# Turning the quantized rows of a feed-forward layer by DMA instead of on TensorE

## The chip, the cores and the metric

The kernel runs on one core of a Trainium2 chip. A core has TensorE (PE, matrix products; its weight loads are listed apart as PEld), VectorE (DVE), ScalarE (ACT), GpSimd (POOL), and SyncE (SP), which here only issues DMAs. The metric is the device time of one execution in microseconds, as a median over runs.

## The reference

Two layers act on an array x of 8 x 256 rows of 512 numbers, each as an attention and a feed-forward with a residual:

```
x = x + attention0(layernorm(x), ctx, ctx)
x = x + ffn0(layernorm(x), w1, w2, w3)        # the stage of this change
x = x + attention1(layernorm(x), ctx, ctx)
x = x + experts1(layernorm(x))                # 32 experts, 4 per row, and a shared one
```

ffn0 is a feed-forward whose activations are rounded to 8-bit integers, row by row, and whose weights are rounded to -1, 0 and 1:

```
act_quant(x)    : scale = 127 / max(|x| over the row); round(x * scale), clipped, / scale
weight_quant(w) : scale = 1 / mean(|w|);  round(w * scale) clipped to -1..1, / scale
bitlinear(x, w) = act_quant(x) @ weight_quant(w).T
ffn0(x) = bitlinear(silu(bitlinear(x, w1)) * bitlinear(x, w3), w2)
```

w1 and w3 lead from 512 to 1408 columns, w2 leads back from 1408 to 512.

## The kernel before

The 2048 rows are 16 tiles of 128 rows (`NT` is 16), rows on the partitions. All of x stays in SBUF in 16 tiles `X[i]`. A product on TensorE contracts over the partitions, so the rounded rows of a tile must be turned (their columns put on the partitions, in blocks of 128) before each of the two products of the feed-forward.

`layer0_attention` (lines 196 to 398) first does the attention of layer 0, tile by tile, in the loop at line 377. In its last two rounds it already starts the feed-forward of the first two tiles: `ffn_input` (416) and `ffn_turned` (432), whose results go into `g.begun`. Its PSUM pool `a0ps` fills all eight banks; the tag `t`, one bank, takes the transposes.

`ffn_input(i)` normalizes tile i of x (`xn`, line 424) and rounds it. `quantize` (401) does this in four steps: maximum of each row on DVE (406), its scale and the inverse of it (408, 410), scaling and rounding on ACT by adding a large constant (411), and on DVE the subtraction of that constant with a cast to bf16 (412). The result is `xq`, 128 x 512, with the scales `s13`.

`ffn_turned` turns `xq` in four blocks by `transpose_blocks` (104): one TensorE transpose per block (108) into PSUM, then one ACT copy (436) into `xqT` in SBUF, of which there are three buffers.

`layer0_ffn` (440 to 486) is the loop over tiles. `hidden` makes the 1408 columns in three chunks of 512, 512 and 384: for each chunk four products with w1 into `p1` and four with w3 into `p3` (453), Silu on ACT (457), and the product of the two on DVE (458) into `h`. Then `quantize` rounds `h` to `hq`, 128 x 1408 in bf16. `output` turns `hq` in eleven blocks by TensorE into two PSUM tiles, copies them by ACT (472) to `hqT`, multiplies with w2 in eleven products into `py` (475), and adds the result to x (476).

The PSUM pool `f0ps` has two buffers each of `p1`, `p3`, `py` and `t`, eight banks together.

The loop at line 480 is written in the order hidden(n-2), output(n-4), ffn_turned(n): two tiles lie between a tile's input and its hidden part, and two between that and its output. The order on each engine is not exactly the written one. A planner orders the instructions ahead of time: on each engine, what is ready by its reckoning and stands first in the written order goes next, and buffers that are still in use hold an instruction back. It is free to take instructions of the next stage early: so the norms of layer 1 (`layernorm`, 67, called at 573) and loads for later stages (`load_early`, 1121, on SP's queue) appear within this stage. Once ordered, each engine and each queue works strictly in order.

Of the kernel before, what the change touches and what calls it, by code (L numbers as in the profile page):

```python
# [19 lines left out]
F32 = mybir.dt.float32  # L20
BF16 = mybir.dt.bfloat16
# [9 lines left out]
P = 128  # L31
D = 512
KD = D // P
# [3 lines left out]
NT = T // P  # L37
# [4 lines left out]
FF = 1408  # L42
NF = FF // P
# [60 lines left out]
def transpose_blocks(g, pool, src, n, dtype, ident, tag):  # L104

    pt = pool.tile([P, n, P], dtype, tag=tag, name="pt")
    for k in range(n):
        g.nc.tensor.transpose(pt[:, k, :], src[:, k * P : (k + 1) * P], ident)
    return pt
# [86 lines left out]
def layer0_attention(g, tc, cp, qpool):  # L196


    nc = g.nc
# [4 lines left out]
    with ExitStack() as ctx:  # L204
        wp = ctx.enter_context(tc.tile_pool(name="a0w", bufs=1, reuse_waits="tile"))
        work = ctx.enter_context(tc.tile_pool(name="a0work", bufs=2, reuse_waits="tile"))
        ps = ctx.enter_context(tc.tile_pool(name="a0ps", bufs=1, space=PSUM, reuse_waits="tile"))
# [5 lines left out]
        for c in range(NCH):  # L213
            for i in range(c * CH // P, (c + 1) * CH // P):
                nc.sync.dma_start(out=g.X[i], in_=g.x[i * P : (i + 1) * P, :])
            nc.sync.dma_start(
                out=g.ctxT[c],
                in_=g.ctxT_d[:, c * CH : (c + 1) * CH].rearrange("(k p) t -> p k t", p=P),
# [93 lines left out]
        def gate(i):  # L312
            c, o = divmod(i * P, CH)
            pw = ps.tile([P, D], F32, tag="pq", name="pw", bufs=2)
            for k in range(KD):
                nc.tensor.matmul(  # L316
                    pw, lhsT=xnT[c][:, k, o : o + P], rhs=wg[:, k, :], start=k == 0, stop=k == KD - 1
                )
            return pw
# [7 lines left out]
        def centered(i):  # L327


            raw = work.tile([P, D], F32, tag="raw", name="raw")  # L330
            nc.sync.dma_start(out=raw, in_=g.ctx[i * P : (i + 1) * P, :])
            by_head = raw.rearrange("p (h d) -> p h d", d=HD1)
            mean = g.small.tile([P, H1], F32, tag="mean", name="mean")
            nc.vector.tensor_reduce(mean, by_head, AX.X, ALU.add)
            nc.vector.tensor_scalar(mean, mean, 1.0 / HD1, None, ALU.mult)
            nc.gpsimd.tensor_sub(by_head, by_head, mean.unsqueeze(2).to_broadcast([P, H1, HD1]))
            nc.gpsimd.memset(by_head[:, :, HD1 - 1 :], 1.0)
            nc.gpsimd.dma_start(out=g.vc_d[i * P : (i + 1) * P, :], in_=raw)

        def attended(i):  # L340

            b, j = divmod(i, 2)
            v = V[b]
            po = ps.tile([P, D], F32, tag=f"s{j}", name="po")
            for h in range(H0):
                cols = slice(h * HD0, (h + 1) * HD0)
                late = AT[h][:, S:] if j else g.ones[:, :P]
                nc.tensor.matmul(
                    po[:, cols], lhsT=AT[h][:, j * P : (j + 1) * P], rhs=v[0][:, cols], start=True, stop=False
                )  # L350
                nc.tensor.matmul(po[:, cols], lhsT=late, rhs=v[1][:, cols], start=False, stop=True)
            y = work.tile([P, D], F32, tag="y", name="y")
            layernorm(g, y, po, g.eps["gn"])
            nc.gpsimd.tensor_mul(y, y, gam)
            nc.gpsimd.tensor_add(y, y, bet)
            return y

        def gated(pw, y):
            wy = work.tile([P, D], F32, tag="wy", name="wy")
            nc.vector.scalar_tensor_tensor(wy, pw, 0.0, y, ALU.max, ALU.mult)  # L360
            return wy

        def turned(wy):
            wyT = work.tile([P, KD, P], F32, tag="wyT", name="wyT")
            nc.scalar.copy(wyT, transpose_blocks(g, ps, wy, KD, F32, g.ident, "t"))  # L365
            return wyT
# [10 lines left out]
        for i in range(NT + 1):  # L377
            if i < NT:
                y = attended(i)
                centered(i)  # L380
            if i:
                wyT = turned(wy.pop(i - 1))
            if i == NT - 1:
                g.begun.append(ffn_turned(g, ps, *begun))
            if i < NT:
                wy[i] = gated(pw, y)
            if i + 1 < NT:
                pw = gate(i + 1)
            if i:
                output(i - 1, wyT)  # L390
            if i == NT:
                g.begun.append(ffn_turned(g, ps, *begun))
            if NT - 2 <= i < NT:
                begun = ffn_input(g, work, i - NT + 2)
            if i % 2 and i // 2 + 2 < B:
                for j in range(2):
                    values(i // 2 + 2, j)
            ternary.round()
# [17 lines left out]
def ffn_input(g, work, i):  # L416

    nc = g.nc
    if i % 4 == 0:
        group = g.rs[:, i : i + 4]  # L420
        nc.scalar.activation(group, g.mv[:, i : i + 4, 1], AF.Sqrt, bias=g.eps["ln"])
        nc.vector.reciprocal(group, group)
    xn = work.tile([P, D], F32, tag="y", name="xn")
    nc.vector.tensor_scalar(xn, g.X[i], g.mv[:, i, 0:1], g.rs[:, i : i + 1], ALU.subtract, ALU.mult)
    xq = work.tile([P, D], BF16, tag="xq", name="xq")
    ix = quantize(g, xq, xn, xn)
    s13 = g.fin.tile([P, 2], F32, tag="s13", name="s13", bufs=4)
    nc.vector.tensor_scalar(s13, g.iw[:, :2], ix, None, ALU.mult)
    return xq, s13


def ffn_turned(g, ps, xq, s13):

    pt = transpose_blocks(g, ps, xq, KD, BF16, g.identb, "t")
    xqT = g.fin.tile([P, KD, P], BF16, tag="xqT", name="xqT", bufs=3)
    g.nc.scalar.copy(xqT, pt)  # L436
    return xqT, s13[:, 0:1], s13[:, 1:2]


def layer0_ffn(g, tc):  # L440
    nc = g.nc
    w1, w3, w2 = g.wq
    chunks = [(c, min(c + 512, FF)) for c in range(0, FF, 512)]
    with tc.tile_pool(name="f0work", bufs=2, reuse_waits="tile") as work, tc.tile_pool(name="f0ps", bufs=2, space=PSUM, reuse_waits="tile") as ps:

        def hidden(i, xqT, s1, s3):
            h = work.tile([P, FF], F32, tag="h", name="h")
            for a, z in chunks:
                p1 = ps.tile([P, 512], F32, tag="p1", name="p1")
                p3 = ps.tile([P, 512], F32, tag="p3", name="p3")  # L450
                for pp, w in ((p1, w1), (p3, w3)):
                    for k in range(KD):
                        nc.tensor.matmul(  # L453
                            pp[:, : z - a], lhsT=xqT[:, k, :], rhs=w[:, k, a:z], start=k == 0, stop=k == KD - 1
                        )
                sg = work.tile([P, 512], F32, tag="sg", name="sg")
                nc.scalar.activation(sg[:, : z - a], p1[:, : z - a], AF.Silu, scale=s1)
                nc.vector.scalar_tensor_tensor(
                    h[:, a:z], p3[:, : z - a], s3, sg[:, : z - a], ALU.mult, ALU.mult
                )  # L460
            hq = work.tile([P, FF], BF16, tag="hq", name="hq", bufs=3)
            ih = quantize(g, hq, h, h)
            s2 = work.tile([P, 1], F32, tag="s2", name="s2", bufs=4)
            nc.vector.tensor_mul(s2, ih, g.iw[:, 2:3])
            return hq, s2

        def output(i, hq, s2):
            hqT = work.tile([P, NF, P], BF16, tag="hqT", name="hqT")
            for a in range(0, NF, 8):
                n = min(8, NF - a)  # L470
                pt = transpose_blocks(g, ps, hq[:, a * P :], n, BF16, g.identb, "t")
                nc.scalar.copy(hqT[:, a : a + n, :], pt)
            py = ps.tile([P, D], F32, tag="py", name="py")
            for f in range(NF):
                nc.tensor.matmul(py, lhsT=hqT[:, f, :], rhs=w2[:, f, :], start=f == 0, stop=f == NF - 1)
            nc.vector.scalar_tensor_tensor(g.X[i], py, s2, g.X[i], ALU.mult, ALU.add)


        xq, hq = dict(enumerate(g.begun)), {}
        for n in range(len(xq), NT + 4):  # L480
            if 0 <= n - 2 < NT:
                hq[n - 2] = hidden(n - 2, *xq.pop(n - 2))
            if n >= 4:
                output(n - 4, *hq.pop(n - 4))
            if n < NT:
                xq[n] = ffn_turned(g, ps, *ffn_input(g, work, n))


def split3(nc, pool, x, name):
# [928 lines left out]
```

## Time and profile before

| what | value |
|---|---|
| time, median of 3 runs | 1166.49 us (1163.6 to 1167.83) |
| the profiled execution's own time | 1169.08 us |
| its span | 1167.3 us |
| TensorE busy | 1047.1 us, 90% |
| VectorE, ScalarE, GpSimd busy | 548.9, 435.7, 385.2 us |
| layer-0 feed-forward, first product to last update of x | 244.7 to 388.7 us of the span |
| TensorE clock granted, mean | 0.965 of full speed |

Times in the trace are counted from the start of the span. A line of a timeline gives start and duration in us, the engine, the line of the kernel and the operation, what it writes and reads, the sizes, and how many like it were merged; in square brackets stands how long the engine had been idle before and what released it. SPq is SP's DMA queue. In a table of stretches each engine has its busy time and its number of instructions. TensorE's products overlap, so that the duration of one is longer than the time from its start to the start of the next.

### The profile page before, as it was taken

The page shows a single profiled execution, that of the slowest core. Times are in us where ns is not written, and L with a number is a line of the kernel's source. Part 1 is how long each engine was busy: PE and PEld are TensorE (multiplying, and loading weights), DVE is VectorE, ACT ScalarE, POOL GpSimd, SP SyncE. Part 2 cuts the span into 40 slices and gives each one's busy share as a digit, 9 for nine tenths or more (in the row PEclk, how much of TensorE's full clock was granted, in tenths as well). Part 3 has the DMA queues.
Part 4 walks back from the last instruction along what each step waited for, and adds up shares of the span by engine and source line. Part 5 has one row for each costly group of instructions (what it writes and reads, how often), then busy time and mean ns, then how long its engine had stood idle before and what let it go on. Part 6 is the DMA issues. An engine that isn't in the chain of part 4 may idle for free. (4 is left out here: it accounts for less than half of the span.)

```text
span 1167.3 us, 14991 instructions
## 1 busy us (share of the span) xinstructions
PE 1047.1 (90%) x5411; PEld 626.5 (54%) x5428; DVE 548.9 (47%) x1403; ACT 435.7 (37%) x740; POOL 385.2 (33%) x355
## 2 busy tenths in 40 slices
PE   7978899969999575999899989999999999999994
PEld 5745466534445233655544445555555666667672
DVE  6445645568987634798863971212121111221210
ACT  4445324158977234778651101111222222211111
POOL 0144422210001400255471133444544555544422
PEclk9989899999999797999899999999999999999998
DMA  9676411110000001112022345667776777878772
GB/s 352 252 251 203 140 54 45 30 37 1 1 1 13 4 1 55 42 58 75 29 75 97 127 132 143 164 183 178 199 186 178 189 193 198 223 221 225 218 188 35
DMA packets 68645, 145.81 MB, mean 125 GB/s; under 512 B 6761, under 2 KB 9449, under 8 KB 68537
## 3 DMA queue, kind: packets, MB, share of 16 engines
q1 hardware_dynamic: 49456, 98.97, 25.7%
q0 software_dynamic: 18672, 45.58, 17.7%
q8 instruction: 45, 0.74, 0.3%
q14 instruction: 40, 0.32, 0.1%
q10 hardware_dynamic: 432, 0.20, 0.1%
HBM read 111.24 MB, written 33.49 MB: 124 GB/s over the span
## 5 line engine op out<-in xcount | busy, mean ns | idle before, releaser
L1229 POOL DMA_INDIRECT out_x<-eo,to x84 | 130.0, 1547 | 227.5 <-ACT eo L1255 212.6
L1185 PE MATMUL po<-w,act 128*128 128x512 f32 (+3 forms) x448 | 139.5, 494 | 5.3 <-DVE act L1174 5.2
L1169 PE MATMUL pg<-xT,w 128*128 128x288 f32 (+7 forms) x512 | 139.7, 416 | 3.9 <-DVE xT L1226 3.9
L1169 PE MATMUL pu<-xT,w 128*128 128x288 f32 (+7 forms) x512 | 136.8, 410 | 0.0
L1173 ACT ACTIVATE sg<-pg 128x288 f32<-128x288 f32 (+8 forms) x68 | 28.9, 425 | 255.8 <-PE pg L1169 238.3
L1255 ACT ACTIVATE eo<-po,slotw 128x512 f32<-128x512 f32 (+3 forms) x112 | 64.2, 578 | 160.0 <-PE po L1185 157.7
L1169 PEld LDWEIGHTS pg<-xT,w 128*128 128x128 f32 x512 | 95.2, 191 | 33.5 <-DVE xT L1226 7.3
L1169 PEld LDWEIGHTS pu<-xT,w 128*128 128x128 f32 x512 | 97.2, 190 | 29.1 <-issue 3.0
L1226 DVE COPY xT<-pt 128x512 f32<-128x512 f32 (+3 forms) x84 | 48.9, 619 | 133.6 <-PE pt L1225 119.1
L1220 DVE SCALAR_TENSOR_TENSOR of<-xg,is_rank 128x32 f32<-128x32 f32 (+3 forms) x84 | 15.8, 188 | 188.8 <-DMA xg<-h_d,tok_of 188.3
L1210 POOL DMA_INDIRECT xg<-h_d,tok_of x84 | 82.5, 983 | 63.2 <-DVE free L1091 35.5
L1185 PEld LDWEIGHTS po<-w,act 128*128 128x128 f32 (+3 forms) x448 | 55.6, 161 | 80.5 <-issue 50.1
L453 PE MATMUL p<-wq,xqT 128*128 128x512 bf16 (+1 forms) x382 | 84.7, 367 | 2.2 <-ACT xqT L436 1.8
L682 DVE SCALAR_TENSOR_TENSOR ct<-pqk,xe 128x768 f32<-128x768 f32 x64 | 58.2, 950 | 26.2 <-PE pqk L678 19.1
L316 PE MATMUL pw<-wg,xnT 128*128 128x512 f32 x128 | 61.5, 626 | 0.0
L371 PE MATMUL pz<-wo,wyT 128*128 128x512 f32 x128 | 57.8, 594 | 2.4 <-ACT wyT L365 2.4
L453 PEld LDWEIGHTS <-xqT 128*128 128x128 bf16 x384 | 36.9, 99 | 37.6 <-issue 3.8
L659 ACT ACTIVATE xe<-pd 128x512 f32<-128x512 f32 x96 | 54.1, 598 | 7.9 <-issue 6.0
L1225 PE MATMUL pt<-ident,xg 128*128 128x128 f32 (+4 forms) x336 | 46.5, 270 | 11.0 <-DVE xT L1226 9.5
L1174 DVE TENSOR_TENSOR act<-pu,sg 128x288 f32<-128x288 f32 (+8 forms) x68 | 31.9, 474 | 42.6 <-PE pu L1169 42.2
L1225 PEld LDWEIGHTS pt<-ident,xg 128*128 128x128 f32 (+4 forms) x336 | 35.3, 141 | 30.7 <-issue 17.2
L740 POOL TENSOR_TENSOR hid<-hid,rsq 128x1024 f32<-128x1024 f32 x8 | 15.3, 1913 | 104.7 <-ACT nm L725 86.7
(294 smaller groups left out, 1759.7 us busy)
## 6 DMA issues: line engine op xcount, KB each, us to landing
w<-in_w SPq DMA_DIRECT2D x32, 1024.0 KB
w<-in_w SPq DMA_DIRECT2D x32, 512.0 KB
wst<-in_w1T SPq DMA_DIRECT2D x8, 704.0 KB
wst<-in_w3T SPq DMA_DIRECT2D x8, 704.0 KB
wst<-in_w2T SPq DMA_DIRECT2D x6, 768.0 KB
x<-in_x SPq DMA_DIRECT2D x16, 256.0 KB
ctxT<-in_ctxT_d SPq DMA_DIRECT2D x4, 1024.0 KB
raw<-in_ctx SPq DMA_DIRECT2D x16, 256.0 KB
```

The costliest lines, as they stand in the source:

```text
L316: nc.tensor.matmul(pw, lhsT=xnT[c][:, k, o : o + P], rhs=wg[:, k, :], start=k == 0, stop=k == KD - 1)
L371: nc.tensor.matmul(pz, lhsT=wyT[:, k, :], rhs=wo[:, k, :], start=k == 0, stop=k == KD - 1)
L453: nc.tensor.matmul(pp[:, : z - a], lhsT=xqT[:, k, :], rhs=w[:, k, a:z], start=k == 0, stop=k == KD - 1)
L659: nc.scalar.activation(out, pd, AF.Exp)
L682: nc.vector.scalar_tensor_tensor(ct[:, r : r + 2, :], pqk[:, :, : S + P], 1.0 / math.sqrt(HD1), xe[:, r : r + 2, :], ALU.mult, ALU.mult,)
L1169: nc.tensor.matmul(pp[:, :n], lhsT=w[:, k, cols], rhs=xT[:, k, :n], start=k == 0, stop=k == KD - 1)
L1185: nc.tensor.matmul(po[h * n : (h + 1) * n, :cols], lhsT=act[:, m, j * P : j * P + n], rhs=w[:, m, h * cols : (h + 1) * cols], start=m == 0 ...
L1210: nc.gpsimd.indirect_dma_start(out=xg[:n], out_offset=None, in_=h_d, in_offset=bass.IndirectOffsetOnAxis(ap=g.tok_of[:n, r, j : j + 1], ax ...
L1225: nc.tensor.transpose(pt[:, k, :n], xg[:n, k * P : (k + 1) * P], g.ident[:n, :n])
L1226: nc.vector.tensor_copy(xT, pt[:, :, :n])
L1229: return nc.gpsimd.indirect_dma_start(out=g.out, out_offset=bass.IndirectOffsetOnAxis(ap=rows, axis=0), in_=eo, in_offset=None, compute_op ...
L1255: nc.scalar.activation(eo[:n, at : at + cols], po, AF.Copy, scale=w[:n, j : j + 1])
```

## The change

The transposes of `xq` and of `hq` on TensorE, and the ACT copies that took them from PSUM to SBUF, are replaced by one DMA each, issued from SP, which reads the rounded rows in SBUF and writes them turned into SBUF. That of `hq` is issued at the end of `hidden` and no longer in `output`, so the buffers shift: two of `hq` and three of `hqT` in place of three and two. The two PSUM banks of `t` in this stage go to `p1` and `p3`, which have three buffers each. In the attention's loop the turning of the first two tiles follows directly on their rounding; before, it was placed one round later by hand.

```diff
@@ -380,18 +380,14 @@
                 centered(i)
             if i:
                 wyT = turned(wy.pop(i - 1))
-            if i == NT - 1:
-                g.begun.append(ffn_turned(g, ps, *begun))
             if i < NT:
                 wy[i] = gated(pw, y)
             if i + 1 < NT:
                 pw = gate(i + 1)
             if i:
                 output(i - 1, wyT)
-            if i == NT:
-                g.begun.append(ffn_turned(g, ps, *begun))
             if NT - 2 <= i < NT:
-                begun = ffn_input(g, work, i - NT + 2)
+                g.begun.append(ffn_turned(g, *ffn_input(g, work, i - NT + 2)))
             if i % 2 and i // 2 + 2 < B:
                 for j in range(2):
                     values(i // 2 + 2, j)
@@ -429,11 +425,10 @@
     return xq, s13
 
 
-def ffn_turned(g, ps, xq, s13):
-
-    pt = transpose_blocks(g, ps, xq, KD, BF16, g.identb, "t")
+def ffn_turned(g, xq, s13):
+
     xqT = g.fin.tile([P, KD, P], BF16, tag="xqT", name="xqT", bufs=3)
-    g.nc.scalar.copy(xqT, pt)
+    g.nc.sync.dma_start_transpose(out=xqT, in_=xq)
     return xqT, s13[:, 0:1], s13[:, 1:2]
 
 
@@ -446,8 +441,8 @@
         def hidden(i, xqT, s1, s3):
             h = work.tile([P, FF], F32, tag="h", name="h")
             for a, z in chunks:
-                p1 = ps.tile([P, 512], F32, tag="p1", name="p1")
-                p3 = ps.tile([P, 512], F32, tag="p3", name="p3")
+                p1 = ps.tile([P, 512], F32, tag="p1", name="p1", bufs=3)
+                p3 = ps.tile([P, 512], F32, tag="p3", name="p3", bufs=3)
                 for pp, w in ((p1, w1), (p3, w3)):
                     for k in range(KD):
                         nc.tensor.matmul(
@@ -458,18 +453,15 @@
                 nc.vector.scalar_tensor_tensor(
                     h[:, a:z], p3[:, : z - a], s3, sg[:, : z - a], ALU.mult, ALU.mult
                 )
-            hq = work.tile([P, FF], BF16, tag="hq", name="hq", bufs=3)
+            hq = work.tile([P, FF], BF16, tag="hq", name="hq")
             ih = quantize(g, hq, h, h)
             s2 = work.tile([P, 1], F32, tag="s2", name="s2", bufs=4)
             nc.vector.tensor_mul(s2, ih, g.iw[:, 2:3])
-            return hq, s2
-
-        def output(i, hq, s2):
-            hqT = work.tile([P, NF, P], BF16, tag="hqT", name="hqT")
-            for a in range(0, NF, 8):
-                n = min(8, NF - a)
-                pt = transpose_blocks(g, ps, hq[:, a * P :], n, BF16, g.identb, "t")
-                nc.scalar.copy(hqT[:, a : a + n, :], pt)
+            hqT = work.tile([P, NF, P], BF16, tag="hqT", name="hqT", bufs=3)
+            nc.sync.dma_start_transpose(out=hqT, in_=hq)
+            return hqT, s2
+
+        def output(i, hqT, s2):
             py = ps.tile([P, D], F32, tag="py", name="py")
             for f in range(NF):
                 nc.tensor.matmul(py, lhsT=hqT[:, f, :], rhs=w2[:, f, :], start=f == 0, stop=f == NF - 1)
@@ -483,7 +475,7 @@
             if n >= 4:
                 output(n - 4, *hq.pop(n - 4))
             if n < NT:
-                xq[n] = ffn_turned(g, ps, *ffn_input(g, work, n))
+                xq[n] = ffn_turned(g, *ffn_input(g, work, n))
```

## The prediction

> **What bounds the kernel now.** I read the page's head first: one execution spans 1167.3 us and TensorE is busy 90% of it.
>
> ```profile
> span 1167.3 us, 14991 instructions
> PE 1047.1 (90%) x5411; PEld 626.5 (54%) x5428; DVE 548.9 (47%) x1403; ACT 435.7 (37%) x740; POOL 385.2 (33%) x355
> ```
>
> The chain that ended last is of no use here: all its longest pieces lie past 845 us, in the experts of layer 1, and this change is in the feed-forward of layer 0, between 230 and 389 us. So I asked for busy time by stretches, one tile of 128 rows each (columns: stretch, its length, busy us and instructions of PE, PEld, DVE, ACT, POOL, TensorE clock, DMA share, GB/s).
>
> ```profile
> 252.80:261.20 8.40, 2.75 (x16) 1.46 (x16) 8.17 (x22) 4.56 (x6) 0.00 (x0) 0.86 0.00 1
> ...
> 302.50:311.10 8.60, 8.41 (x53) 4.15 (x52) 7.83 (x18) 8.54 (x12) 0.00 (x0) 1.00 0.00 1
> ...
> 352.10:360.20 8.10, 8.05 (x54) 4.14 (x52) 6.75 (x15) 6.10 (x8) 0.00 (x0) 1.00 0.00 0
> ```
>
> From 261.2 to 375.4 us fourteen tiles take 114.2 us, 8.16 each. Most are bounded by TensorE (8.05 of 8.10 us). Four early ones take 8.6 because ScalarE is full too (8.54), with two table loads of 1.28 us per tile for the norms of layer 1 that the planner put in between. VectorE is next, 6.65 to 7.93 us per tile. The DMA engines do nothing. One tile in the timeline (start, duration, engine):
>
> ```profile
> 359.56 0.78 PE L108 MATMUL pt<-identb,hq 128*128 128x128 bf16 x11
> 360.17 1.24 PE L453 MATMUL p<-wq,xqT 128*128 128x512 bf16 x5
> 361.27 2.55 PE L475 MATMUL py<-wq,hqT 128*128 128x512 bf16 x10
> 363.66 2.32 PE L453 MATMUL p<-wq,xqT 128*128 128x512 bf16 x10
> 364.58 0.89 DVE L412 TENSOR_SCALAR hq<-h 128x1408 bf16<-128x1408 f32 x1
> 365.39 0.42 DVE L412 TENSOR_SCALAR xq<-xn 128x512 bf16<-128x512 f32 x1
> 365.87 0.40 PE L108 MATMUL pt<-identb,xq 128*128 128x128 bf16 x4
> 366.11 1.68 PE L453 MATMUL p<-wq,xqT 128*128 128x512 bf16 x9
> 366.31 0.58 ACT L436 COPY xqT<-pt 128x512 bf16<-128x512 bf16 x1 [0.19 <-PE pt L108]
> 367.62 0.78 PE L108 MATMUL pt<-identb,hq 128*128 128x128 bf16 x11
> 368.27 1.39 ACT L472 COPY hqT<-pt 128x1024 bf16<-128x1024 bf16 x2 [0.46 <-PE pt L108]
> ```
>
> See two things. TensorE never rests, and its transposes cost it 0.61 us (359.56 to 360.17) and 0.24 us (365.87 to 366.11) per tile. And xq of tile 15, finished at 365.81, is wanted by that tile's first product right behind the transposes, at 368.24: the margin is 2.4 us, though the loop is written with two tiles between them, because VectorE takes xq in written order behind hq of tile 13.
>
> **What the Trainium skill says.** "VectorE: DVE Perf Modes", The three transpose paths: 1309 ns for one 128x128 bf16 block through the DMA, 390 ns on TensorE. The trace disagrees on TensorE: 219 ns each, pipelined to some 60. "DMA: Bandwidth & Descriptors", Latency and other measured facts: a transposing DMA moved 261 GB/s in one kernel; its Anatomy of one DMA gives about 2.0 us fixed per DMA. The trace has no transposing DMA; a small one agrees on the fixed part:
>
> ```profile
> 443.56 0.34 SPq L615 DMA_DIRECT2D parts_d<-sp  x1
> ...
> 445.95 0.28 SPq L638 DMA_DIRECT2D right<-parts_d  x1
> ```
>
> The second reads what the first wrote: 2.39 us from issue to landing, or less.
>
> **The change part by part.**
>
> 1. Removed from TensorE: 15 transposes per tile, 0.61 + 0.24 = 0.85 us. Removed from ScalarE: the copies hqT (1.39) and xqT (0.58), 1.97 us. VectorE keeps everything.
>
> 2. What is next. Per tile TensorE falls to 8.05 - 0.85 = 7.2, ScalarE to 8.54 - 1.97 = 6.6 at most; VectorE stays. Taking in each of the fourteen stretches the larger of 7.2 and VectorE's busy time (7.42, 7.64, 7.93, 7.92, 7.83, 7.93, 7.45, 7.64, 7.29, then 7.2 four times, about 6.5 for the last) gives 104.4 us: at most 9.8 us fall away. Two engines level with each other do not both run full; I take two thirds, -6.5 us, and 0 and -9.8 as ends.
>
> 3. Added: 16 DMAs of 128x512 (131 KB) and 16 of 128x1408 (360 KB) on SP's queue. Estimate from the DMA page: 2.0 + 131/261 = 2.5 us and 2.0 + 360/261 = 3.4 us. The pair arrives within 1 us (hq ends 0.34 us before xq), so xq's data wait behind hq's: 365.47 + 3.4 + 0.5 = 369.4, a latency L of 3.5 us from the end of xq. Bounds: 1.3 us (one block's price), and 1.3 us for each of 15 blocks one after another, 19.6 us per tile. I take 3.5.
>
> 4. Does L show? A loop over two tiles decides. From the last product of tile 13 (359.72) through its h, maximum, rounding and then xq of tile 15 (365.81) is 6.1 us; then L; then the 24 products of tile 15 and an output in between: tile 14 took 360.17 to 367.79, less 0.24 for transposes, 7.4. So (13.5 + L)/2 per tile; at L = 3.5 that is 8.5, worse than now. If a tile's three chunks follow each other, with the output's eleven products (2.35 us) outside the loop, (11.1 + L)/2 = 7.3. The third bank of p1 and p3 allows just this: with two, chunk 0 of a tile waits for chunk 1 of the tile before. Written order puts `hidden` ahead of `output`, and xq depends on nothing in this stage but buffers (two of xn and xq, three of xqT), so any idle VectorE lets it run ahead. I therefore take it as hidden; if that cover is gone, rival 2 prices it.
>
> 5. Start. The first product stands at 244.72, after 0.67 us idle for the copy of tile 1's xqT:
>
> ```profile
> 243.66 0.39 PE L108 MATMUL pt<-identb,xq 128*128 128x128 bf16 x4
> 244.72 6.64 PE L453 MATMUL p<-wq,xqT 128*128 128x512 bf16 x31 [0.67 <-ACT xqT L436]
> ```
>
> Without both it starts at 243.66: -1.1 us. But then tile 2: xq ends at 259.47, its first product starts at 261.22, 1.75 us later; with L = 3.0 (hq of tile 0 ended 0.34 us earlier, some of it moved) it is +1.25. This is the second row of the stretches above, where TensorE works 2.75 of 8.4 us and VectorE is full.
>
> 6. End. hq of tile 15 ends at 382.09, the transposes wait for TensorE until 383.59, and py starts at 385.36, 3.27 us later. By DMA: 3.4 us, less 0.4 because VectorE's update of tile 13 no longer stands in front of hq. -0.3.
>
> 7. SP's queue. Loads of `raw` and of the weights were all issued before 182 us; what is left around the first transposes is gw, nw, sg_w at 227 and su_w, sd_w at 243.9. su_w waits on a buffer until then; a transpose of tile 1 queued behind it would land near 247.5, and tile 1's products start near 248. POOL's queue gets nothing. Buffers: hq from three to two, hqT from two to three, same sizes: 0. The layer-1 front (VectorE and GpSimd stand 8.4 us in each other's way there) moves with the end of the stage: 0, with +-2 us if the planner shuffles it.
>
> Sum: -6.5 - 1.1 + 1.25 - 0.3 = -6.7 us. The profiled execution took 1169.1 us (span 1167.3 and 1.8 around it), so 1162.4 for the like; the median of the runs is 2.6 us lower: 1159.8.
>
> **The rivals.**
>
> 1. *Covered, as above*: 1159.8, own range 1150 to 1163. For: idle DMA engines, a full TensorE. Against: the 2.4 us margin.
>
> 2. *xq comes late.* The wait for the copy is replaced by a wait for the DMA, place: first product of each tile. At the order of today the loop decides above L = 2 x 8.16 - 13.5 = 2.8 us. L = 3: 8.25 per tile, +1.3, with start and end about +1: 1167. L = 4: 8.75, +8.3 for fourteen tiles, +2.2 at tile 2, -1.1 at the start: 1176. For: FIFO behind the nearly three times larger hq. Against: the third banks.
>
> 3. *The DMA can't keep pace.* It becomes the bound above 8.16/15 = 0.54 us per block. At the skill's 1.309 us per block a tile takes 19.6 us, 16 tiles 314 instead of 144: about 1337. For: the only block price there is. Against: it is less than the 2 us fixed price, so it looks like one DMA's latency and not its pace.
>
> 4. *More than the stage*: TensorE and VectorE reach the floor (-9.8), or the layer-1 front also gets shorter: 1152.
>
> **How the numbers follow.** Covered 0.48 (0.42 beyond 0.5%, 0.06 within); rival 4 0.10, faster; xq late but about even (L near 3) 0.17, of it 0.15 within and 0.02 slower; xq late with L of 4 and more 0.15, slower; DMA-bound 0.10, slower. Faster 0.52, same 0.21, slower 0.27; 0.5% is 5.8 us, about what a measurement of this kernel can tell from no change (the three runs lie 4.2 us apart). The range 1149 to 1181 leaves out rival 3 and the tips of 2 and 4.
>
> **What would show it.** Right: no L108 with identb and no copies L436, L472; per-tile stretches of 7.2 to 7.9 us with TensorE and VectorE above 95%; landing of the transposes in 2.5 to 4 us; first product near 243.7. Wrong: products (L453) waiting for DMA xqT, DMA share above half in this stage, or stretches of 8.2 us and more with VectorE below 7 us.

## The result and the profile after

The changed kernel takes 1182.4 us (median of four executions, 1177.0 to 1182.9) against 1166.1 for the kernel before: a ratio of 1.0131, interval 1.0096 to 1.0166. It is slower, where 1159.8 us was predicted. A second set of executions gave 1177.6 us, ratio 1.0123 (1.0072 to 1.0174). The profiled execution took 1182.87 us.

The head of the page of the changed kernel:

```profile
span 1181.0 us, 14577 instructions
PE 1038.7 (88%) x5176; PEld 613.7 (52%) x5188; DVE 547.8 (46%) x1403; ACT 402.4 (34%) x690; POOL 385.7 (33%) x355
```

TensorE is busy 8.4 us less and ScalarE 33.3 us less (435.7 before), and yet the span grew by 13.7 us. Busy time by stretches (stretch, length, then PE, PEld, DVE, ACT, POOL, TensorE clock, DMA share, GB/s) shows where; the first four rows are single tiles, the last is the fourteen tiles in a row that took 114.2 us before:

```profile
254.95:263.35 8.40, 0.58 (x2) 0.11 (x2) 7.51 (x23) 4.53 (x4) 0.00 (x0) 0.63 0.31 59
302.40:310.92 8.52, 7.62 (x36) 3.43 (x36) 7.09 (x19) 6.97 (x8) 0.00 (x0) 1.00 0.31 59
310.92:323.28 12.36, 7.60 (x35) 3.35 (x36) 11.67 (x27) 6.12 (x7) 0.00 (x0) 0.95 0.21 40
349.89:358.29 8.40, 7.38 (x35) 3.25 (x36) 7.10 (x16) 3.88 (x5) 0.00 (x0) 1.00 0.31 59
263.35:388.40 125.05, 107.27 (x472) 47.61 (x482) 96.18 (x206) 62.65 (x77) 0.07 (x1) 0.93 0.31 53
```

Over the fourteen tiles no engine is full any more. A late tile still takes 8.4 us with TensorE at 7.38 and VectorE at 7.10. Two early ones take 12.4; there VectorE is busy almost throughout (11.67 of 12.36 us), for a reason that is given below. What TensorE and its weight loads waited for in this stage (waited in total, times, longest, us):

```profile
PEld L467 <- DMA hqT<-hq: 35.9, 12, 8.8
PE py L467 <- DMA hqT<-hq: 29.5, 11, 8.4
PEld L448 <- DMA xqT<-xq: 6.2, 11, 1.8
PE p L448 <- DMA xqT<-xq: 1.3, 1, 1.3
```

Read quickly, this says that the output's hqT is late. The timeline of one late tile (start, duration, engine, line) says otherwise:

```profile
350.97 0.69 ACT L452 ACTIVATE sg<-p,s 128x512 f32<-128x512 f32 x1 [4.54 <-PE p L448]
351.55 1.55 ACT L407 ACTIVATE h<-h,eps_magic,qs 128x1408 f32<-128x1408 f32 x1
353.13 0.90 DVE L408 TENSOR_SCALAR hq<-h 128x1408 bf16<-128x1408 f32 x1 [0.48 <-ACT h L407]
353.94 0.42 DVE L408 TENSOR_SCALAR xq<-xn 128x512 bf16<-128x512 f32 x1
354.09 1.39 SPq L461 DMA_TRANSPOSE hqT<-hq  x1
355.57 1.44 SPq L431 DMA_TRANSPOSE xqT<-xq  x1
357.73 0.60 PE L467 MATMUL py<-wq,hqT 128*128 128x512 bf16 x2 [0.97 <-DMA hqT<-hq]
358.29 4.93 PE L448 MATMUL p<-wq,xqT 128*128 128x512 bf16 x24
```

The planner put a product or two of py just ahead of the next tile's 24 products. hqT and xqT leave as a pair and land 0.6 us apart, so py's product takes the wait, and the wait list names hqT. The 24 products behind it could not have started before xqT. From the end of xq (354.36) to the first product that uses it (358.29) is 3.93 us. Of the fourteen tiles from tile 2 on, eleven start 3.83 to 3.96 us after their xq ended: for those the arrival of xqT sets the start. The other three (3, 6 and 9) start 8.5 us and more after it, and each follows a tile that had to wait in this way.

The same is seen on the DMA engines. These are 40 slices of 0.15 us from 354 to 360 us: busy tenths, and what they moved.

```profile
DMA  0000000039999999999999993000000000050000
GB/s 0 0 0 0 0 0 0 0 53 207 220 217 208 213 198 222 217 191 186 227 190 212 222 215 77 4 0 0 0 0 0 0 0 0 0 109 0 0 0 0
```

Data begin to move 1.1 us after the issue of hq's DMA, and both transfers (491 KB) pass in one piece of 2.5 us at some 210 GB/s. Half a microsecond later TensorE starts. xq's 131 KB pass last, behind the 360 KB of hq.

**Where the 13.7 us are**, in parts that meet end to end (us):

| part | before | after | difference |
|---|---|---|---|
| up to the stage's first product | 244.72 | 244.69 | 0.0 |
| first product to tile 2's first | 16.50 | 18.66 | +2.2 |
| fourteen tiles | 114.2 | 125.0 | +10.8 |
| last hidden product to last py | 12.5 | 15.7 | +3.2 |
| layer 1's front, up to gs (L582, now L574) | 42.8 | 40.9 | -1.9 |
| all after it | 736.6 | 736.1 | -0.5 |

The stage from its first product to its last py is 143.2 us before and 159.4 after. Start and end of the stage after the change:

```profile
241.16 3.70 PE L371 MATMUL pz<-wo,wyT 128*128 128x512 f32 x8 [0.92 <-ACT wyT L365]
244.69 9.67 PE L448 MATMUL p<-wq,xqT 128*128 128x512 bf16 x47
262.77 0.61 PE L467 MATMUL py<-wq,hqT 128*128 128x512 bf16 x1 [8.41 <-DMA hqT<-hq]
...
391.11 2.55 PE L467 MATMUL py<-wq,hqT 128*128 128x512 bf16 x11 [0.80 <-DMA hqT<-hq]
394.36 1.32 DVE L408 TENSOR_SCALAR hq<-h 128x1408 bf16<-128x1408 f32 x1
399.32 4.76 PE L467 MATMUL py<-wq,hqT 128*128 128x512 bf16 x11 [5.67 <-DMA hqT<-hq]
```

At the start nothing stands between the attention's last product and the first one here: the 1.1 us are gone, but in this execution the work ahead came 1.0 us later, so the sum did not move. At the end the last py waits 5.67 us for hqT, and then its eleven products take 4.76 us where the same eleven took 2.55 at 391.11. TensorE's granted clock was 0.52 in those 4.76 us and 1.00 at 391.11.

### The profile page after: what moved, and what is told of

It is laid out like the page before. It is cut to its first block, busy times and chain, and to the rows that moved or that the text cites. A ratio compares the mean times of both kernels' runs of the same rounds, so it can differ in the third digit from the quotient of the medians.

```text
span 1181.0 us, 14577 instructions
## 1 busy us (share of the span) xinstructions
PE 1038.7 (88%) x5176; PEld 613.7 (52%) x5188; DVE 547.8 (46%) x1403; ACT 402.4 (34%) x690; POOL 385.7 (33%) x355
## 4 chain that ended last, share of the span: by engine, by line
PE 53%; DMA 14%; DVE 11%; issue 9%; POOL 6%; ACT 6%; SPq 0%; POOLq 0%; DVEq 0%; ACTq 0%
PE po L1177 9%; PE pg L1161 8%; PE pu L1161 7%; PE p L448 5%; DMA out_x<-eo,to 3%; PE pz L371 3%; PE pw L316 3%; DMA hqT<-hq 3%; DMA xg<-h_d,tok_of 2%; POOL out_x L1221 2%; PE pt L1217 2%; DMA raw<-in_ctx 2%; DVE xT L1218 1%; PE pqk L666 1%; PE pt L108 1%
## 5 line engine op out<-in xcount | busy, mean ns | idle before, releaser
L467 PE MATMUL py<-wq,hqT 128*128 128x512 bf16 x171 | 44.1, 399 | 30.4 <-DMA hqT<-hq 29.5
```

## The theory, its rival, and the experiments

**Loop theory.** xq(n+2) is made behind hq(n) on VectorE, so the products of one tile decide when xq of a later one is ready. The latency L = 3.9 us of xq's DMA lies in that loop and nothing covers it. From the timeline above the loop of a late tile closes within *one* tile: first product of tile n+1 at 349.89; sg of its first chunk on ScalarE at 350.97 (+1.08); the rounding of h(n), which stands behind that sg in ScalarE's queue, at 351.55 (+0.58); hq at 353.13 (+1.58); xq's end at 354.36 (+1.23); first product of tile n+2 at 358.29 (+3.93). Sum 8.40 us, the period measured.

**Output theory** (the rival). What TensorE is recorded as waiting for is the cause: hqT lands too late for the output product, and xqT is no trouble.

Medians in us, ratios to the kernel before in the same set of runs, and the stage's length in the profiled execution:

| kernel | time | ratio and interval | stage |
|---|---|---|---|
| hq by DMA alone | 1157.9 | 0.9939 (0.9917 to 0.9961) | 136.8 |
| xq by DMA alone | 1168.4 | 1.0030 (1.0014 to 1.0046) | 148.3 |
| changed, p1 and p3 in two buffers | 1177.2 | 1.0105 (1.0079 to 1.0130) | 159.0 |
| changed, input written early | 1149.0 | 0.9871 (0.9843 to 0.9899) | 127.9 |
| changed, xq's DMA twice | 1187.2 | 1.0170 (1.0137 to 1.0203) | 166.4 |
| input early, xq's DMA twice | 1149.9 | 0.9863 (0.9826 to 0.9899) | 130.0 |
| changed, hq's DMA written later | 1180.1 | 1.0110 (1.0077 to 1.0143) | 158.8 |
| before, input written early | 1160.6 | 0.9956 (0.9928 to 0.9984) | 139.0 |
| input early, two buffers | 1150.1 | 0.9876 (0.9848 to 0.9905) | 127.5 |
| input early, output later | 1141.3 | 0.9782 (0.9730 to 0.9833) | 121.5 |
| changed, hq's DMA from ScalarE | 1214.5 | 1.0409 (1.0384 to 1.0433) | 197.8 |
| changed, again | 1177.6 | 1.0123 (1.0072 to 1.0174) | 157.2 |

### One half of the change alone

The kernel before, with only hq turned by DMA (xq by TensorE as before, p1 and p3 in two buffers; the transposes and copies in `output` fall away, as in the change):

```diff
...
-            return hq, s2
+            hqT = work.tile([P, NF, P], BF16, tag="hqT", name="hqT", bufs=3)
+            nc.sync.dma_start_transpose(out=hqT, in_=hq)
+            return hqT, s2
...
```

> Only hq is turned by DMA; xq goes through TensorE and ScalarE as in the kernel before, and p1, p3 have two banks each. Loop theory (what costs the time is xq's turned copy arriving 3.9 us after its rounding, in the loop over two tiles): with xq back on TensorE its latency is 1.8 us, TensorE still saves 0.61 us per tile, about 7.6 us per tile instead of 8.16, so 1158 to 1164. Output theory (TensorE stands in order behind a product of the output that waits for hqT): hqT still comes by DMA, so it stays slow, 1175 or more.

and with only xq turned by DMA:

```diff
-    pt = transpose_blocks(g, ps, xq, KD, BF16, g.identb, "t")
-    g.nc.scalar.copy(xqT, pt)
+    g.nc.sync.dma_start_transpose(out=xqT, in_=xq)
```

> Only xq is turned by DMA; hq goes through TensorE as before. Loop theory: without hq's DMA ahead in the queue the latency of xq falls from 3.9 to about 2.5 us, which gives (13.5 + 2.5)/2 = 8.0 us per tile at the order of before: 1163 to 1172. Output theory: no wait for hqT by DMA is left, TensorE is bound at 8.05 - 0.24 = 7.8 us per tile: 1160 to 1164.

Measured: 1157.9 and 1168.4 us. With hq alone the same hqT arrives by the same DMA, the kernel is *faster* by 0.6%, and in its list of waits (waited in total, times, longest, us) one wait of TensorE for hqT is left in the whole stage, at its end:

```profile
PE py L472 <- DMA hqT<-hq: 3.4, 1, 3.4
```

So the output theory falls: hqT by DMA alone costs the tiles nothing. With xq alone the 0.24 us of transposes and 0.58 us of copy are saved, and it is no faster: xq's DMA then has no hq ahead of it and is still waited for, as that kernel's list of waits shows:

```profile
PE p L452 <- DMA xqT<-xq: 6.9, 8, 1.8
```

The time lies in the loop theory's range, but its working does not hold here: from the first product of tile 2 to that of tile 15 (258.34 to 369.76) a tile takes 8.57 us on average, where 8.0 was worked out for L = 2.5. Not all of it is xq's: the waits for the ACT copies of hqT grew as well, from 3.1 to 6.0 us.

### The third buffers

```diff
-                p1 = ps.tile([P, 512], F32, tag="p1", name="p1", bufs=3)
-                p3 = ps.tile([P, 512], F32, tag="p3", name="p3", bufs=3)
+                p1 = ps.tile([P, 512], F32, tag="p1", name="p1", bufs=2)
+                p3 = ps.tile([P, 512], F32, tag="p3", name="p3", bufs=2)
```

> The changed kernel with two buffers of p1 and p3 instead of three (two PSUM banks stay unused). If the third banks are what lets the 24 products of a tile follow each other, and so keeps an output out of the loop, it gets slower: 1185 to 1195. If the third banks only led the planner to bunch tiles (three at a time, with 4.7 us of wait), it gets faster: 1170 to 1178. If they don't matter, 1179 to 1185.

Measured: 1177.2 us. That is the changed kernel's own second figure (1177.6), and its late tiles keep the period (8.4 us). The third buffers neither help nor harm here; in the late tiles the 24 products follow one another without them too, and the two long early tiles are there as well (13.0 us each).

### More lead: the input written ahead of the hidden step

In the loop over tiles, with xqT in four buffers (two for the tiles begun earlier, which come from another pool):

```diff
+            if n < NT:
+                xq[n] = ffn_turned(g, *ffn_input(g, work, n), pool=work)
             if 0 <= n - 2 < NT:
                 hq[n - 2] = hidden(n - 2, *xq.pop(n - 2))
...
-            if n < NT:
-                xq[n] = ffn_turned(g, *ffn_input(g, work, n))
```

> The changed kernel with one change of written order: the input of tile n (normalizing, rounding, turning) is written ahead of hidden of tile n-2 and no longer behind it and the output, with four buffers of xqT. Loop theory: xq no longer stands behind hq of the tile two before, the loop is cut, 7.3 to 7.9 us per tile: 1156 to 1166. Output theory: products of the output still wait for hqT in order, no gain: 1178 to 1185.

Measured: 1149.0 us, 1.3% below the kernel before, and below what either theory expected. Late tiles of this kernel:

```profile
343.81 0.42 DVE L408 TENSOR_SCALAR xq<-xn 128x512 bf16<-128x512 f32 x1
343.96 1.38 SPq L461 DMA_TRANSPOSE hqT<-hq  x1
344.84 4.92 PE L448 MATMUL p<-wq,xqT 128*128 128x512 bf16 x23
345.43 1.45 SPq L431 DMA_TRANSPOSE xqT<-xq  x1
349.59 2.54 PE L467 MATMUL py<-wq,hqT 128*128 128x512 bf16 x11
351.96 4.92 PE L448 MATMUL p<-wq,xqT 128*128 128x512 bf16 x24
```

The period is 7.12 us (344.84 to 351.96), TensorE's own work, and xq of the tile that starts at 351.96 was done by 344.2: 7.7 us of lead over a latency of 3.9. TensorE's waits for hqT fall from 29.5 us to 8.2 in three places.

Whether the order alone brings this gain was tried on the kernel before, with the same edit:

> The kernel before (TensorE's transposes), with the input written one tile earlier as in the early variant of the changed kernel and four buffers of xqT. If the gain of that variant is the DMA's, TensorE stays the bound at 8.05 us per tile and only the wait of 4.6 us at tile 2 can go: 1159 to 1165. If it is the order's alone: 1147 to 1154.

Measured: 1160.6 us, ratio 0.9956. So the four combinations read: the change costs 1.2 to 1.3% in the old order, and in the early order it brings 0.9871 / 0.9956 = 0.9915, 0.85%. The DMA-turned rows are worth at least what the prediction hoped for (0.6%) once a tile more of lead covers them.

### More latency

A second, identical DMA of xq, which SP issues when the first has landed:

```diff
     g.nc.sync.dma_start_transpose(out=xqT, in_=xq)
+    g.nc.sync.dma_start_transpose(out=xqT, in_=xq)
```

> The changed kernel with the DMA that turns xq issued twice into the same tile, the second waiting on SP for the first: xq's latency grows by one DMA, about 2.7 us (from the issue at 355.57 to the first product at 358.29 in the changed kernel), from 3.9 to 6.6 us. Loop theory: half of it per tile, 1.35 us, 19 us over fourteen tiles and some 3 at the start: 1198 to 1210. Output theory: hqT comes no later, so 1180 to 1186.

and the same with the input written early:

> The kernel with the early input, with the same doubled DMA of xq. Loop theory: where xq is taken a tile earlier there is one more tile (7.1 us) of slack, which covers 2.7 us more: the same as with the early input alone, 1147 to 1154. If the latency still counts there, about 1165 to 1170.

Measured: 1187.2 and 1149.9 us. With the lead the added latency costs no time that could be told from nothing, as the loop theory says; one wait of 5.2 us for xqT stands at tile 2, and the steady tiles keep their 7.1 us. Without it the sign is right, but the size is not: the kernel is 5 to 10 us slower than the changed one where 16 to 28 were expected. The queue of SP shows that the latency did grow, by about as much as was meant:

```profile
347.52 1.38 SPq L462 DMA_TRANSPOSE hqT<-hq  x1
349.01 1.43 SPq L431 DMA_TRANSPOSE xqT<-xq  x1
351.72 1.19 SPq L432 DMA_TRANSPOSE xqT<-xq  x1
```

The second DMA writes the same tile and starts 2.7 us after the first. The end of xq to its first product is now 6.3 to 7.0 us instead of 3.9. What gave way is the order: the planner laid the tiles out differently. In several tiles the rounding of h(n) now stands *ahead* of the next tile's sg on ScalarE (353.88 and 356.05 us), so the loop runs over two tiles there and L counts half. From tile 2 to tile 15 a tile takes 9.73 us on average against 9.24 in the changed kernel. The run bears out that L is in the loop; it does not measure how steep the loop is.

### The place in the queue

First in the written order alone, with hq's DMA behind the next input:

```diff
             if n < NT:
                 xq[n] = ffn_turned(g, *ffn_input(g, work, n))
+            if 0 <= n - 2 < NT:
+                hq[n - 2] = turned(*hq[n - 2])
```

(`turned` holds the two lines that allocate hqT and issue its DMA, taken out of `hidden`.)

> The changed kernel with the DMA of hq written behind that of xq (of the tile two later), so that on SP's queue xq no longer stands behind hq's 1.5 us of issue. Loop theory: xq's latency falls from 3.9 to about 2.8 us, half of 1.1 us per tile, 8 us over fourteen tiles: 1171 to 1178. Output theory: hqT lands some 2 us later than now, so it gets slower: 1190 to 1210.

Measured: 1180.1 us. It tells nothing: in the trace SP still issues hq's DMA 1.5 us ahead of xq's in every late tile, so the planner did not follow the written order there. So hq's DMA was given to another queue:

```diff
-            nc.sync.dma_start_transpose(out=hqT, in_=hq)
+            nc.scalar.dma_start_transpose(out=hqT, in_=hq)
```

> The changed kernel with hq's transposing DMA issued from ScalarE's queue instead of SP's, so that xq's DMA no longer stands behind hq's issue on SP (xq's issue began 1.48 us after hq's in the changed kernel's late tiles). Theory A (loop, and the queue is part of L): L falls from 3.9 to about 2.5 us, a tile of the late stretch from 8.4 to (16.8 - 1.5) / 2 = 7.7 us, so about 10 us off the changed kernel's time over 14 tiles: 1169 to 1176 us. Theory B (the place in the queue is worth nothing, since the DMAs' own work is serial or the issue costs ScalarE as much as SP's queue cost before): 1178 to 1187 us, the late tiles still at 8.3 us or more.

Measured: 1214.5 us, 4% slower than before, outside both expectations. One tile, DMA issues, and the first products:

```profile
350.69 0.42 DVE L408 TENSOR_SCALAR xq<-xn 128x512 bf16<-128x512 f32 x1
350.81 1.28 ACTq L461 DMA_TRANSPOSE hqT<-hq  x1
...
354.46 1.19 SPq L431 DMA_TRANSPOSE xqT<-xq  x1
356.95 1.20 PEld L448 LDWEIGHTS <-xqT 128*128 128x128 bf16 x7 [3.71 <-DMA xqT<-xq]
...
358.03 0.69 ACT L452 ACTIVATE sg<-p,s 128x512 f32<-128x512 f32 x1 [5.25 <-PE p L448]
```

xq ends at 351.11, but SP issues its DMA at 354.46. The wait list of SP's queue names the reason (its 131 us are mostly time in which SP had no xq to send; what counts is what ended the waits):

```profile
SPq L431 <- DMA hqT<-hq: 131.1, 12, 17.0
```

The two queues do not work side by side: the program holds xq's DMA on SP until hq's has landed. This is what the Trainium skill asks for in "DMA: Bandwidth & Descriptors", Silent corruption: two transposing streams in flight at once: the later stream has to wait for the earlier one's full completion. The trace agrees, at 3.35 us of waiting here. So the edit made L longer, 5.84 us, instead of shorter. It is thereby a test of the loop after all, and with the order on ScalarE kept: sg of the next tile stands ahead of the rounding here too. For the tile from 345.11 to 356.95 the steps of the loop are, in the order used above, 1.98, 0.59, 2.22, 1.21 and 5.84 us, together the 11.84 us of that tile. It is 3.4 us longer than the 8.40: the 1.9 us of L in full and not in half, 0.9 from products at a lower clock after the wait (0.50 granted in its first 2 us), and 0.6 from norm statistics on VectorE. From tile 2 to tile 15 a tile takes 11.9 us on average (9.9 to 14.6) against 9.24. The stage grew by 38 to 41 us over the changed kernel's two profiles. xq's DMA alone takes 2.49 us from its issue to the first product (354.46 to 356.95); of the 3.93 us in the changed kernel, about 1.4 are hq's doing.

> The changed kernel itself beside the run with hq's DMA on ScalarE's queue, on the same chip: 1179 to 1184 us, ratio 1.010 to 1.017, as in its first runs; the yardstick for the small differences of the runs with two banks (1177) and with hq's DMA written behind xq's (1180). If it comes at 1177 to 1180, those two are no different from it.

Measured: 1177.6 us; single executions of the changed kernel in both sets lie between 1177 and 1186. The two buffers (1177.2) and the DMA written later (1180.1) are no different from it.

### Is there more in it

The early order (the input written early) with two buffers of p1 and p3:

> The changed kernel with the layer-0 input written one tile ahead of the hidden step, as in the earlier run of that order (1149.0 us, ratio 0.987), and with the first two products' PSUM tiles in two buffers instead of three. Theory A (loop: with the lead the stage stands on TensorE's own 7.1 us a tile and two buffers are enough to feed it): 1147 to 1153 us, ratio 0.984 to 0.990. Theory B (the third buffers carry part of the gain, since a pair of products then waits for the evictions and the multiply on ScalarE and VectorE, about 1 us more a tile over 14 tiles): 1158 to 1166 us, ratio 0.993 to 1.000.

Measured: 1150.1 us against 1149.0: the third buffers are worth nothing here either. Then, against the early order, one tile more of lead on both sides, with buffers to match (xqT five, hqT four, s13 and s2 six):

```diff
-        for n in range(len(xq), NT + 4):
+        for n in range(len(xq), NT + 6):
             if n < NT:
                 xq[n] = ffn_turned(g, *ffn_input(g, work, n), pool=work)
-            if 0 <= n - 2 < NT:
-                hq[n - 2] = hidden(n - 2, *xq.pop(n - 2))
-            if n >= 4:
-                output(n - 4, *hq.pop(n - 4))
+            if 0 <= n - 3 < NT:
+                hq[n - 3] = hidden(n - 3, *xq.pop(n - 3))
+            if n >= 6:
+                output(n - 6, *hq.pop(n - 6))
```

> The changed kernel with the input written early (as in the run of 1149.0 us), and besides with the hidden step three and the output step six tiles behind the start, and xqT, hqT and the rounded-row tiles in one or two more buffers each. That run still showed 8.2 us of waits for hqT in three places. Theory A (these are the latency of hq's DMA, and a tile more of lead takes them away, with nothing in their place): 1140 to 1146 us, ratio 0.978 to 0.984. Theory B (the time is kept, since the fill and the drain of the stage grow by a tile's lead, or TensorE then waits for something else): 1147 to 1155 us, ratio 0.984 to 0.991.

Measured: 1141.3 us, ratio 0.9782 (0.9730 to 0.9833), the best of all. Input and output got their lead together here, so what each of them brings is not known. The stretch of its steady tiles, and the end of the stage:

```profile
265.70:349.08 83.38, 82.96 (x404) 40.11 (x411) 81.89 (x185) 56.52 (x69) 0.10 (x1) 1.00 0.35 68
349.08:362.89 13.81, 11.24 (x43) 4.42 (x42) 7.42 (x11) 3.90 (x5) 8.12 (x13) 0.88 0.48 87
```

TensorE is busy 82.96 of 83.38 us and VectorE 81.89: here two engines level with each other do both run full. TensorE waits for hqT once more, 2.6 us in the drain.

## Why the prediction was wrong, step by step

- **Step 1** (0.85 us of TensorE and 1.97 of ScalarE per tile fall away) was right: 15 transposes and their copies are gone.
- **Step 2** (the next bound, and two thirds of 9.8 us) was right as a floor and wrong as a forecast. The fourteen tiles took 125.0 us instead of 107.7; with more lead TensorE does reach 7.1 us a tile.
- **Step 3** (L = 3.5 us) was a little small: 3.93 measured. The fixed part was about right, though the 2.0 us were borrowed: in the Trainium skill, "DMA: Bandwidth & Descriptors", Anatomy of one DMA, they are fitted to DMAs issued from GpSimd, and these go out from SP. An estimate from the runs is 1.9 us (2.49 less 131 KB at 210 GB/s, and 3.58 from issue to py at the end of the stage less 360 KB). The engines moved some 210 GB/s where the page's 261 was taken. L = 2.5 for xq alone, as estimated, was right (2.49).
- **Step 4 is where it failed**: "I therefore take it as hidden". Nothing covered L: its 3.93 us stood in full in the loop of a late tile (8.40 us), and the fourteen tiles got 10.8 us longer instead of 6.5 shorter. The sum in front of that sentence was nearly right. I had written the loop, found 8.5 us per tile at L = 3.5, and then argued it away: the third banks would let a tile's three chunks follow each other, which takes the output out of the loop, and xq could run ahead when VectorE idles. The first came true (24 products in one row) and did not help, and it does not need the third banks. The second did not: each engine works through its queue in order, VectorE makes xq(n+2) behind hq(n) there, and an idle VectorE waits with it.

  And the contiguous chunks cost something that the formula (11.1 + L)/2 lacked. The 6.1 us from a tile's last product to the next xq became 7.96 in a late tile (346.40 to 354.36): the next tile's products come sooner, so its sg goes ahead of this tile's rounding on ScalarE (0.8 us), VectorE updates x first (0.5), and two sg and two multiplies lie behind the last product instead of one (0.6). By the two-tile sum, (4.93 + 7.96 + 3.93)/2 = 8.41, the period measured. But 0.81 of the 7.96 are spent waiting for that sg (qs is there at 350.74, the rounding starts at 351.55); without it the two-tile loop would allow 8.0. The loop that binds in the late tiles is the one through the sg, over one tile, where L counts in full. That reading rests on the trace and on the run with hq's DMA on ScalarE's queue; putting the rounding ahead of the sg alone was not tried.

Most of the loss lies in two early tiles, which take 12.4 us each: tile 4 (280.66 to 293.01) and tile 7 (310.92 to 323.28). From the first product of tile 2 to that of tile 15, thirteen tiles take 120.1 us instead of 107.0. Of these 13.1 us, 8.2 are in the two; 2.5 are in the two tiles behind them, whose products begin at a lower clock after a wait of 4.7 us (granted clock 0.73 and 0.72 over these tiles); and 2.3 are in the other nine, 8.49 us each against 8.23. (The products of tile 15 itself then take 2.2 us less, since no output lies among them; hence the 10.8 for all fourteen.) The timeline of the changed kernel shows the end of tile 3 and tile 4:

```profile
276.86 1.28 ACT L75 ACT_TABLE_LOAD   x1
...
278.47 1.28 ACT L452 ACT_TABLE_LOAD   x1
...
279.76 0.58 ACT L452 ACTIVATE sg<-p,s 128x384 f32<-128x384 f32 x1
...
281.74 0.69 ACT L452 ACTIVATE sg<-p,s 128x512 f32<-128x512 f32 x1 [1.39 <-PE p L448]
283.46 0.69 ACT L452 ACTIVATE sg<-p,s 128x512 f32<-128x512 f32 x1 [1.04 <-PE p L448]
284.98 0.58 ACT L452 ACTIVATE sg<-p,s 128x384 f32<-128x384 f32 x1 [0.82 <-PE p L448]
285.46 1.55 ACT L407 ACTIVATE h<-h,eps_magic,qs 128x1408 f32<-128x1408 f32 x1
...
288.69 0.42 DVE L408 TENSOR_SCALAR xq<-xn 128x512 bf16<-128x512 f32 x1
```

ScalarE takes two table loads for a norm of layer 1 ahead of the last sg of tile 3. That sg ends 8.13 us after the tile's first product (272.21); in tile 9, which has no such loads, it ends after 5.10. Then all three sg of tile 4 stand ahead of the rounding of h of tile 3, and VectorE, busy 11.91 of 12.35 us, takes the multiplies and the maximum of tile 4 ahead of hq of tile 3. xq ends 8.45 us after the tile's first product at 280.66, and with 3.9 of latency the next tile starts at 293.01. Tiles 6 and 7 are the same. The tile behind tile 9 takes 8.42 us. So the loads, which the prediction counted as busy time of ScalarE alone, cost latency in a loop without slack. This is read from the trace; the stage without layer 1's norms was not tried.

- **Step 5** (start: -1.1, then +1.25 at tile 2) was right in the first part, as far as the wait for the copy is gone. Tile 2 came 2.2 us later, since L was 3.91 there (259.44 to 263.35) instead of 3.0: the term was mis-sized. hq of tile 0 ended only 0.33 us ahead and none of its data had moved before xq was done.
- **Step 6** (end: -0.3) failed: +3.2 us. hqT takes 3.64 us from hq's end to py (395.68 to 399.32), near the 3.4 estimated and 0.4 more than the transposes and copies took. Lost besides are 0.6 us before hq's end and 2.2 us in the products after the wait, at about half the clock; that a longer idle stretch slows the products behind it was not in the sum.
- **Step 7** (queue and front: nothing, +-2 us) was right: layer 1's front is 1.9 us shorter, and the loads on SP did not delay the first product (244.69 us).

**Rivals.** Rival 2, "xq comes late", is what happened, and in the right place (first product of each tile). That its number fits, 1176 us at L = 4 against 1177 to 1182 measured, is in part luck: it had 8.75 us in every tile, and what came was 8.4 in the late ones and 12.4 in two. Its threshold, L = 2.8 us, is not borne out: with xq alone L was 2.5 where xqT set the start (367.24 to 369.76), and the tiles were still longer than before. I gave rival 2 a chance of 0.32 in all; 2.4 us of margin against an estimated latency of 3.5 should have decided for it. Rival 3, the DMA as the bound, is refuted by a DMA share of 0.31 in the stage: the fifteen blocks of a tile pass in 2.5 us, 0.17 us each, where it had 1.309. Of rival 4, TensorE and VectorE at the floor is what the early order gave.

## What to carry to other kernels

A DMA that replaces work on an engine trades busy time for latency. Before it is called hidden, find the loop through the in-order queues in which it lies, from the trace, and compare its latency with the margin there (2.4 us here against 3.9); buffers do not give lead if the order of the queues does not. Give the producer a tile more of lead in the written order together with the change: this turned 1.3% slower into 1.3% faster, and a second tile, for the output too, made it 2.2%. And a wait list names the instruction that stood in front, not always the transfer that was missed: look at what was queued right behind it.

## What the runs showed of the hardware

- A transposing DMA from SBUF to SBUF holds SP's queue 1.2 to 1.5 us, whether it moves 131 or 360 KB; data start some 1.1 us after the issue and pass at about 210 GB/s. From issue to use it is 2.5 us for 128x512 alone, and 3.6 for 128x1408.
- Two transposing DMAs on different queues ran one after the other, since SP waits for the landing of the other queue's (3.35 us in the tile shown); two on one queue passed without a gap.
- After 5.67 us of idle time eleven products of py took 4.76 us, 0.43 each, against 0.23 in a busy stretch; the granted clock was 0.52 and 1.00. "TensorE: Matmul & The Clock Gate", What's actually happening, has a half-speed clock after an idle window of about 3.4 us; the trace agrees.
